# A two-layer graph kernel's head: row split ahead of the edge columns, first weights and packed rows loaded ahead, part of the edge table cleared on GpSimd

## The chip, the cores and the metric

The kernel runs on one core of one Trainium2 chip. A core has TensorE (PE in the profile, its weight loads PEld), VectorE (DVE), ScalarE (ACT), GpSimd (POOL), and SyncE (SP), which here issues DMAs. The metric is the device time of one execution in microseconds, lower is better. The kernel before took 1517.72 us, the median of three runs (1516.66 to 1518.28).

## The reference, cut to what matters

1250 nodes with 512 features pass through two layers. Each layer adds to `x` the sum of a graph branch (messages over 40,000 edges) and an attention branch, then a mixture-of-experts branch. What the change touches is the start of the first layer:

```
xn = layernorm(x)
neigh_mean = segment_sum(xn[src], dst) / max(deg, 1)
h = xn @ W_self.T + neigh_mean @ W_neigh.T + bias          # graph branch
a = layernorm(xn) * g1 + be1                               # attention branch
q = sigmoid(a @ Wq + bq); k = sigmoid(a @ Wk + bk); v = a @ Wv + bv
```

The second layer's graph branch uses the same edges with `edge_weight`. Edges come sorted by `dst`.

## The kernel before, in words

Nodes are handled in `T` = 10 tiles of `P` = 125 rows. The first stage makes five products for each tile: y (normalised x times the neighbour weights), z (times the self weights, plus a row vector), q, k and v (twice normalised x times their weights, plus row vectors). Each product is four matmuls of 128x512 in float32, which the trace shows as eight records.

In the same stage the edges become a dense table `at`, of 128 x 2 x 10 x 1258 float32: for each (source, target) pair the count of edges and the sum of weights. The 40,000 edges are 320 chunks of 125. For each chunk PE multiplies a one-hot matrix of sources (`hs`) with a matrix of targets (`hm`: one-hot, and one-hot times the weight in three bfloat16 parts), and DVE adds the result into 8 columns of `at` (L429). Chunks go in groups of eight: DVE makes `hs` (L387) and the one-hot of `hm` (L394), ACT scales a copy of it by the top part of the weight (L397), POOL by the two low parts (L400).

Before any chunk can start, DVE prepares the edges' columns (L326 to L359). Integer `dst` and `src` become float (`dst_f`, `src_f`); the least target of each chunk is taken (`base`); PE turns `src_f`, `dst_f` and the weights (`rest`) from rows of 500 into columns of 125 (L316), and DVE copies them out (`src_c`, `where`, `wt_e`, L317); ten compares give each edge's source tile (`tile_s`, L350 and L352), and from that come `lo_s`, `inside` and `col_w`. POOL splits the weights into bfloat16 parts (`w_low`, `w_top`, L345 to L349).

The biases and other row vectors come packed in a tensor of 16 rows, loaded three times into the partitions of `full` (L298). DVE splits them into three bfloat16 parts, `row_parts` (`split_rows`, L114 to L118: ten instructions). A row vector is added to a product by one more matmul, of `row_pick` with `row_parts` (L101). The first product that needs it is z of tile 0.

Each tile is normalised by DVE (`normal_rows`: statistics L246 and L247, an inverse root for which ACT takes the square root at L250, `xr` L267, a second root, `hr` L270), and turned on PE (`turn`, L132), from where ACT copies it to `xt` and, scaled, to `ht` (L278, L282). Tile 0 is done ahead of the edges' columns in the program; tile 1 when z of tile 0 begins; then one tile ahead. The statistics are taken for tiles 0, then 1 and 2, then 3 to 5, then 6 to 9 together.

`at` is cleared in 20 pieces of 128x1258, by ACT (L438): eight with `fill(8)` ahead of the loop, the rest four at a time.

PE's order in the product loop is the program's (a manual schedule). The order on the other engines, and on PE ahead of that loop, is made by a scheduler when the program is built, from dependences and its own estimates of time; so an instruction may stand somewhere else than the source suggests, and where an edit moves one, others move too. All loads of this stage are issued by SP, in order, with eight semaphores used in turn: a DMA waits until the one eight places ahead has landed. In the order before, these are x of tile 0 (two parts), `dst`, `src`, `rest`, `cols`, the neighbour weights, the self weights, then the three loads of the packed rows, x of tiles 1 and 2, and the weights of q, k and v.

Of the kernel before, what the change touches and what calls it, by code (L numbers as in the profile page):

```python
# [13 lines left out]
AF = mybir.ActivationFunctionType  # L14
# [21 lines left out]
NA = N + W  # L36
# [25 lines left out]
NROW = 16  # L62
# [8 lines left out]
def gps_two_layer_kernel(ctx: ExitStack, tc: tile.TileContext, x, src, dst, ew, rows, cols,  # L71
                         gw_self, gw_neigh, wq0, wk0, wv0, wo0, w1_0, w2_0, wg, we, be,
                         w_conv, w_lin, wq1, wk1, wv1, wo1, temp, w_r, w1_1, w2_1, b2_1, out):
    nc = tc.nc

    const = ctx.enter_context(tc.tile_pool(name="const", bufs=1))
    ident = const.tile([128, 128], F32, name="ident")
# [7 lines left out]
    row_parts = const.tile([96, D], BF16, name="row_parts")  # L85
    row_pick = const.tile([96, 32], BF16, name="row_pick")
    b2_parts = const.tile([96, D], BF16, name="b2_parts")
    cols_sb = const.tile([128, NCOL], F32, name="cols_sb")
# [5 lines left out]
    srcr = src.rearrange("(r e) -> r e", r=R)  # L94
    dstr = dst.rearrange("(r e) -> r e", r=R)
    ewr = ew.rearrange("(r e) -> r e", r=R)
# [12 lines left out]
    def split_rows(o, full, pool, **kw):  # L109

        piece = pool.tile([96, D], BF16, name="piece", **kw)
        back = pool.tile([96, D], F32, name="back", **kw)
        for i in range(3):
            nc.vector.tensor_copy(piece, full)  # L114
            nc.vector.tensor_copy(o[32 * i:32 * i + NROW, :], piece[32 * i:32 * i + NROW, :])
            if i < 2:
                nc.vector.tensor_copy(back, piece)
                nc.vector.tensor_tensor(full, full, back, ALU.subtract)  # L118
# [70 lines left out]
    at = adj.tile([128, 2, T, NA], F32, name="at")  # L189
# [3 lines left out]
    zero = l0.tile([128, 1], F32, name="zero")  # L193
# [16 lines left out]
    with ExitStack() as phase:  # L210
        gp = phase.enter_context(tc.tile_pool(name="gnn", bufs=1))
        ring = phase.enter_context(tc.tile_pool(name="ring", bufs=2))
# [16 lines left out]
        full = ring.tile([96, D], F32, name="full", tag="o", bufs=5)  # L229
# [43 lines left out]
        def turn(t):  # L273

            xr, hr = pairs[t]
            pt = transposed(ps, xr)
            xt = ring.tile([128, DC, P], F32, name="xt")
            nc.scalar.copy(xt, pt)  # L278
            pt = transposed(ps, hr)
            ht = ring.tile([128, DC, P], F32, name="ht")  # L280
            for c in range(DC):
                nc.scalar.activation(ht[:, c, :], pt[:, c, :], AF.Identity,  # L282
                                     bias=cols_sb[:, C_BE1 + c:C_BE1 + c + 1],
                                     scale=cols_sb[:, C_G1 + c:C_G1 + c + 1])
            turned[t] = xt, ht

        with tc.tile_pool(name="eprep", bufs=1) as ep, \
                tc.tile_pool(name="eps", bufs=2, space=PSUM) as eps:
            dst_i = ep.tile([R, RE], I32, name="dst_i")
            src_i = ep.tile([R, RE], I32, name="src_i")  # L290
            rest = ep.tile([R, RE], F32, name="rest")
            load_x(0)
            nc.sync.dma_start(dst_i, dstr)
            nc.sync.dma_start(src_i, srcr)
            nc.sync.dma_start(rest, ewr)
            nc.sync.dma_start(cols_sb, cols)
            for i in range(3):
                nc.sync.dma_start(full[32 * i:32 * i + NROW, :], rows[:NROW, :])  # L298
            wn_sb, ws_sb, wq_sb, wk_sb, wv_sb = (
                big[:, i * DC * D:(i + 1) * DC * D].rearrange("p (c f) -> p c f", c=DC)  # L300
                for i in range(5))
            for i, (o, w) in enumerate(((wn_sb, gw_neigh), (ws_sb, gw_self), (wq_sb, wq0),
                                        (wk_sb, wk0), (wv_sb, wv0))):
                nc.sync.dma_start(o, w.rearrange("(c p) f -> p c f", p=128))
                if i == 1:
                    load_x(1)
                    load_x(2)
            load_x(3)
            load_x(4)
            normal_rows(0)  # L310
            turn(0)

            def as_columns(o, f):
                pe = eps.tile([CH, NC // R, R], F32, name="pe")
                for j in range(NC // R):
                    nc.tensor.transpose(pe[:, j, :], f[:, j * CH:(j + 1) * CH], ident[:R, :R])  # L316
                nc.vector.tensor_copy(o.rearrange("p (r j) -> p r j", r=R), pe.rearrange("p j r -> p r j"))  # L317

            def chunks(ap):
                return ap.rearrange("r (j e) -> r j e", e=CH)  # L320

            def each_chunk(ap):
                return ap[:, :, None].to_broadcast([R, NC // R, CH])

            dst_f = ep.tile([R, RE], F32, name="dst_f")
            nc.vector.tensor_copy(dst_f, dst_i)  # L326
            src_f = ep.tile([R, RE], F32, name="src_f", tag="f", bufs=3)
            nc.vector.tensor_copy(src_f, src_i)
            src_c = ep.tile([CH, NC], F32, name="src_c")
            as_columns(src_c, src_f)  # L330
            base = ep.tile([R, NC // R], F32, name="base")
            nc.vector.tensor_reduce(base, chunks(dst_f), AX.X, ALU.min)

            nc.vector.tensor_scalar(base, base, 0.0, float(N - 1), op0=ALU.max, op1=ALU.min)
            nc.vector.tensor_copy(base_i, base)
            nc.vector.tensor_tensor(chunks(dst_f), chunks(dst_f), each_chunk(base), ALU.subtract)
            nc.vector.tensor_scalar(base, base, float(W), None, op0=ALU.add)
            out_f = ep.tile([R, RE], F32, name="out_f", tag="f", bufs=3)
            nc.vector.scalar_tensor_tensor(chunks(out_f), chunks(dst_f), float(W), each_chunk(base),
                                           op0=ALU.is_ge, op1=ALU.mult)  # L340
            nc.vector.tensor_add(dst_f, dst_f, out_f)
            as_columns(where, dst_f)
            as_columns(wt_e, rest)
            less = ep.tile([CH, NC], F32, name="less", tag="f", bufs=3)
            nc.gpsimd.tensor_copy(w_low[:, 0, :], wt_e)  # L345
            nc.gpsimd.tensor_copy(w_top, w_low[:, 0, :])
            nc.gpsimd.tensor_tensor(less, wt_e, w_top, ALU.subtract)
            nc.gpsimd.tensor_copy(w_low[:, 0, :], less)
            nc.gpsimd.tensor_tensor(w_low[:, 1, :], less, w_low[:, 0, :], ALU.subtract)  # L349
            nc.vector.tensor_scalar(tile_s, src_c, float(P), None, op0=ALU.is_ge)  # L350
            for t in range(2, T):
                nc.vector.scalar_tensor_tensor(tile_s, src_c, float(t * P), tile_s,  # L352
                                               op0=ALU.is_ge, op1=ALU.add)
            nc.vector.scalar_tensor_tensor(lo_s, tile_s, float(-P), src_c, op0=ALU.mult, op1=ALU.add)
            nc.vector.scalar_tensor_tensor(src_c, tile_s, float(W), where, op0=ALU.mult, op1=ALU.add)
            inside = ep.tile([CH, NC], F32, name="inside", tag="f", bufs=3)
            nc.vector.tensor_scalar(inside, where, float(W), None, op0=ALU.is_lt)
            nc.vector.scalar_tensor_tensor(src_c, src_c, 1.0, inside, op0=ALU.add, op1=ALU.mult)
            nc.vector.tensor_scalar(col_w, src_c, -1.0, None, op0=ALU.add)  # L359


            nc.vector.memset(row_parts, 0.0)
            split_rows(row_parts, full, ring, tag="o", bufs=5)
            for i in range(3):
                nc.vector.tensor_copy(row_pick[32 * i:32 * i + 32, :],
                                      ident[32 * i:32 * i + 32, 32 * i:32 * i + 32])


            worst = ep.tile([R, 1], F32, name="worst")
            nc.vector.tensor_reduce(worst, out_f, AX.X, ALU.max)  # L370
            pr = eps.tile([1, R], F32, name="pr", bufs=1)
            nc.tensor.transpose(pr, worst, ident[:R, :R])
            any_out = ep.tile([1, 1], F32, name="any_out")
            nc.vector.tensor_reduce(any_out, pr, AX.X, ALU.max)
            nc.vector.tensor_scalar(any_out, any_out, 0.0, float(NC), op0=ALU.is_gt, op1=ALU.mult)
            nc.vector.tensor_copy(trips, any_out)
# [54 lines left out]

        fills = [(m, t) for m in range(2) for t in range(T)]

        def fill(n):
            for _ in range(n):
                if fills:
                    m, t = fills.pop()
                    nc.scalar.activation(at[:, m, t, :], zero.to_broadcast([128, NA]), AF.Copy)  # L438

        kinds = ((y_d, 0, wn_sb, None, AF.Copy), (z_d, 0, ws_sb, R_GNN, AF.Copy),  # L440
                 (q_d, 1, wq_sb, R_BQ0, AF.Sigmoid), (k_d, 1, wk_sb, R_BK0, AF.Sigmoid),
                 (v_d, 1, wv_sb, R_BV0, AF.Copy))
        steps, step, chunk = T * len(kinds) * DC, 0, 0
        fill(8)
        with tc.manual_schedule(engines={mybir.EngineType.PE}):
            for t in range(T):
                for n, (d, which, w_sb, row, func) in enumerate(kinds):
# [39 lines left out]
        with tc.tile_pool(name="far", bufs=1) as fr, tc.tile_pool(name="fps", bufs=1, space=PSUM) as ps:  # L487
# [4 lines left out]
            with tc.For_i(0, n_far, 1) as i:  # L492
                i = nc.s_assert_within(i, 0, NC - 1)
# [942 lines left out]
```

## Time and profile before

| what | us |
|---|---|
| median of three runs | 1517.72 |
| the profiled execution | 1515.57 |
| its span, first to last instruction | 1513.9 |
| PE busy | 1389.8 (92%) |
| DVE busy | 586.5 (39%) |
| ACT busy | 404.4 (27%) |
| POOL busy | 199.1 (13%) |
| first edge product starts on PE | 41.86 |

The span is the time between the first and the last instruction in the profile; the execution's time has 1.67 us more around it. Busy shares are means over stages with different limits: in the first 40 us DVE is nearly always busy and PE is not, later it is the other way round. In the lines of the timeline the columns are start, duration, engine, source line, operation, what it writes and reads, and how often; in brackets stands the idle time ahead of it and what ended it. In the lines of waits: who waited, for whom, total us, how often, the longest. In the lines of windows: the stretch, its length, then for PE, PEld, DVE, ACT and POOL the busy us and the number of instructions, then PE's granted clock, the share of time that the DMA engines were busy, and GB/s.

### The profile page before, as it was taken

The numbers are of one execution on the slowest core, as the hardware profiler recorded it, in microseconds if no ns is written. First come the engines' busy times: TensorE is split into PE (matmuls) and PEld (weight loads), VectorE is DVE, ScalarE is ACT, GpSimd is POOL, SyncE is SP. The second block draws the span as 40 slices with busy tenths as digits, with TensorE's granted clock in tenths as the row PEclk, the third lists the DMA queues.
The fourth block names the chain that finished last, engine by engine and source line by source line (L and its number), as shares of the span: only waits on it lengthen the run. The fifth ranks groups of instructions, "written<-read, shape, count | busy, mean of one in ns | idle before, by whom it ended". The sixth has DMA issues, their size and how long they took to land. (4 is left out here: it accounts for less than half of the span.)

```text
span 1513.9 us, 18419 instructions
## 1 busy us (share of the span) xinstructions
PE 1389.8 (92%) x6082; PEld 870.1 (57%) x6082; DVE 586.5 (39%) x1425; ACT 404.4 (27%) x937; POOL 199.1 (13%) x176
## 2 busy tenths in 40 slices
PE   5999999999999699999965898898999999999997
PEld 2445445434544346554534696884767567975673
DVE  8887777689776583343575000000000000000000
ACT  8655455201224322112224111220212012120110
POOL 3345455300000000000005001000000000000000
PEclk9999999999999799999986999999999999999999
DMA  6311111623510130001149446601552106001011
GB/s 224 102 55 57 55 55 48 188 72 91 175 48 8 51 111 1 0 1 41 48 170 348 168 177 235 226 9 46 193 163 76 14 8 231 12 7 14 1 14 15
DMA packets 72716, 134.73 MB, mean 89 GB/s; under 512 B 8280, under 2 KB 9672, under 8 KB 72574
## 3 DMA queue, kind: packets, MB, share of 16 engines
q1 hardware_dynamic: 67646, 122.47, 23.9%
q0 software_dynamic: 4928, 10.43, 3.5%
q8 instruction: 81, 1.33, 0.4%
q14 instruction: 61, 0.50, 0.1%
HBM read 107.27 MB, written 26.38 MB: 88 GB/s over the span
## 5 line engine op out<-in xcount | busy, mean ns | idle before, releaser
L1323 PE MATMUL po<-w,big 128*128 128x512 f32 x576 | 250.1, 592 | 0.0
L1300 PE MATMUL pm<-hts,big 128*128 x960 | 184.7, 355 | 19.4 <-issue 17.0
L1312 DVE TENSOR_SCALAR o<-po,to_gate 128x512 f32<-128x512 f32 (+1 forms) x24 | 17.7, 749 | 453.8 <-PE po L1325 452.6
L1300 PEld LDWEIGHTS pm<-hts,big 128*128 128x128 f32 x960 | 167.0, 196 | 39.1 <-issue 23.8
L1323 PEld LDWEIGHTS po<-w,big 128*128 128x128 f32 x576 | 109.2, 190 | 132.0 <-issue 131.4
L1303 ACT ACTIVATE big<-pm,cols_sb 128x256 f32<-128x256 f32 (+2 forms) x224 | 96.1, 432 | 282.1 <-PE pm L1300 281.8
L1300 PE MATMUL pm<-hts,w 128*128 x832 | 144.7, 336 | 12.7 <-PEq L1383 5.8
L1300 PEld LDWEIGHTS pm<-hts,w 128*128 128x128 f32 x832 | 133.0, 197 | 23.9 <-issue 14.5
L455 PE MATMUL pm<-big,ht 128*125 128x512 f32 x240 | 130.5, 632 | 0.0
L1313 POOL DMA_INDIRECT out_dram<-o,row x24 | 36.9, 1539 | 650.5 <-DVE o L1312 285.2
L429 DVE TENSOR_TENSOR at<-at,pa 128x160 f32 x320 | 102.2, 319 | 41.3 <-PE pa L427 17.8
L400 POOL TENSOR_TENSOR hm<-hm,w_low 125x640 bf16<-125x640 bf16 x80 | 100.3, 1274 | 114.0 <-DVE hm L394 63.3
L123 PE MATMUL pm<-w,at 128*125 128x512 f32 x240 | 114.2, 598 | 0.0
L397 ACT ACTIVATE hm<-hm,w_top 125x80 bf16<-125x80 bf16 x320 | 86.4, 350 | 68.1 <-DVE hm L394 55.1
L633 PE MATMUL pn<-big,at 125*125 125x512 f32 x200 | 89.4, 604 | 3.0 <-DMA big<-q_d 3.0
L455 PE MATMUL pm<-big,xt 128*125 128x512 f32 x160 | 86.8, 633 | 1.2 <-ACT xt L278 1.2
L1303 ACT ACT_TABLE_LOAD x11 | 14.1, 1283 | 255.4 <-PE pm L1300 255.4
L427 PEld LDWEIGHTS <-hs 125*128 125x128 bf16 x640 | 50.8, 97 | 48.8 <-issue 44.0
L424 PE MATMUL pa<-hm,hs 125*128 125x160 bf16 x320 | 64.6, 233 | 12.9 <-DVE at L429 10.9
L424 PEld LDWEIGHTS <-hs 125*128 125x128 bf16 x320 | 31.1, 97 | 67.7 <-issue 38.4
L633 PEld LDWEIGHTS pn<-big,at 125*125 125x125 f32 x200 | 37.5, 191 | 52.5 <-issue 52.5
L427 PE MATMUL pa<-hm,hs 125*128 125x80 bf16 x640 | 64.4, 198 | 0.0
(391 smaller groups left out, 1616.1 us busy)
## 6 DMA issues: line engine op xcount, KB each, us to landing
w<-in_w_dram SPq DMA_DIRECT2D x52, 1024.0 KB
big<-in_w_dram SPq DMA_DIRECT2D x12, 1024.0 KB
x_t<-in_x_dram SPq DMA_DIRECT2D x10, 224.0 KB
xn_d<-xr SPq DMA_DIRECT2D x10, 224.0 KB
y_d<-o SPq DMA_DIRECT2D x10, 224.0 KB
z_d<-o SPq DMA_DIRECT2D x10, 224.0 KB
q_d<-o SPq DMA_DIRECT2D x10, 224.0 KB
k_d<-o SPq DMA_DIRECT2D x10, 224.0 KB
```

The source lines that it names most:

```text
L123: nc.tensor.matmul(ps, lhs[:, c, :], w[:, c, :], start=(c == 0), stop=(row is None and c == DC - 1))
L397: nc.scalar.activation(hm[:, j, 1, :], hm[:, j, 0, :], AF.Copy, scale=w_top[:, g * J + j:g * J + j + 1])
L400: nc.gpsimd.tensor_tensor(hm[:, :, 2 + i, :], hm[:, :, 0, :], w_low[:, i, c8, None].to_broadcast([CH, J, TW]), ALU.mult)
L424: nc.tensor.matmul(pa.rearrange("p k c -> p (k c)"), hs[:, j, :], hm[:, j, 0:2, :].rearrange("p k c -> p (k c)"), start=True, stop=False)
L427: nc.tensor.matmul(pa[:, 1, :], hs[:, j, :], hm[:, j, 2 + i, :], start=False, stop=(i == 1))
L429: add = nc.vector.tensor_tensor(to, to, pa.rearrange("p k (t w) -> p k t w", t=T), ALU.add)
L455: nc.tensor.matmul(pm, lhs[:, c, :], w_sb[:, c, :], start=(c == 0), stop=(row is None and c == DC - 1))
L633: nc.tensor.matmul(pn, at[:P, 0, s, t * P:(t + 1) * P], y[:, s, :], start=(s == 0), stop=(s == T - 1))
L1300: nc.tensor.matmul(pm[:, :width], w1s[e, f // DC][:, c, (f % DC) * 128:(f % DC + 1) * 128], hts[:, c, bass.ds(start, width)], start=(c == ...
L1303: nc.scalar.activation(hid[f][:, :width], pm[:, :width], AF.Gelu, bias=cols_sb[:, C_B11 + e * FC + f:C_B11 + e * FC + f + 1])
L1313: nc.gpsimd.indirect_dma_start(out, bass.IndirectOffsetOnAxis(ap=row[:n], axis=0), o[:n], None, bounds_check=N - 1, oob_is_err=False, comp ...
L1323: nc.tensor.matmul(pm, hid[f][:, s * 128:(s + 1) * 128], w2s[e, f // DC][:, f % DC, :], start=(f == 0), stop=False)
```

## The change

Three things are edited. The load of the neighbour weights is issued right behind x of tile 0, followed by `dst`, `src`, the three loads of the packed rows, the weights of the edges and the columns; before, the neighbour weights came behind all of these but the packed rows. The split of the packed rows, with its clear and the copies into `row_pick`, stands in the program ahead of the edges' columns and not behind them. The first eight of the 20 pieces of `at` are cleared by POOL and not by ACT.

The scheduler's order that follows from it, by the lists of both programs: SP issues the neighbour weights third, then `dst`, `src`, `rest`, `cols`, the self weights and the three packed-row loads, and what follows stays as it was. On DVE the conversions of `dst` and `src` stand behind `hr` of tile 0; the first piece of the split stands behind `worst` (L370), and the rest of the split alternates with `where`, `wt_e` and seven of the compares; the remaining compares, `lo_s`, `inside` and `col_w`, and `xr` of tile 1 come behind the last copy into `row_parts`; `xr` and `hr` of tile 3 come ahead of the first add into `at`. On PE `hr` of tile 0 is turned right behind `xr`, and all of product y of tile 0 stands between the turning of `src_f` and that of `dst_f`. On ACT the root for tiles 1 and 2 stands behind the copy of q of tile 0, with one more load of an activation table on each side, and the second root for them behind 14 scalings of `hm` and the copy of `xt` of tile 1. On POOL the eight clears stand between the clear of `full` and the casts of `w_low`.

```
             load_x(0)
-            nc.sync.dma_start(dst_i, dstr)
-            nc.sync.dma_start(src_i, srcr)
-            nc.sync.dma_start(rest, ewr)
-            nc.sync.dma_start(cols_sb, cols)
-            for i in range(3):
-                nc.sync.dma_start(full[32 * i:32 * i + NROW, :], rows[:NROW, :])
...
                 nc.sync.dma_start(o, w.rearrange("(c p) f -> p c f", p=128))
+                if i == 0:
+                    nc.sync.dma_start(dst_i, dstr)
+                    nc.sync.dma_start(src_i, srcr)
+                    for r in range(3):
+                        nc.sync.dma_start(full[32 * r:32 * r + NROW, :], rows[:NROW, :])
+                    nc.sync.dma_start(rest, ewr)
+                    nc.sync.dma_start(cols_sb, cols)
                 if i == 1:
                     load_x(1)
                     load_x(2)
             load_x(3)
             load_x(4)
             normal_rows(0)
             turn(0)
+
+            nc.vector.memset(row_parts, 0.0)
+            split_rows(row_parts, full, ring, tag="o", bufs=5)
+            for i in range(3):
+                nc.vector.tensor_copy(row_pick[32 * i:32 * i + 32, :],
+                                      ident[32 * i:32 * i + 32, 32 * i:32 * i + 32])
 
             def as_columns(o, f):
...
             nc.vector.tensor_scalar(col_w, src_c, -1.0, None, op0=ALU.add)
 
-            nc.vector.memset(row_parts, 0.0)
-            split_rows(row_parts, full, ring, tag="o", bufs=5)
-            for i in range(3):
-                nc.vector.tensor_copy(row_pick[32 * i:32 * i + 32, :],
-                                      ident[32 * i:32 * i + 32, 32 * i:32 * i + 32])
 
             worst = ep.tile([R, 1], F32, name="worst")
...
-        def fill(n):
+        def fill(n, early=False):
             for _ in range(n):
                 if fills:
                     m, t = fills.pop()
-                    nc.scalar.activation(at[:, m, t, :], zero.to_broadcast([128, NA]), AF.Copy)
+                    if early:
+                        nc.gpsimd.memset(at[:, m, t, :], 0.0)
+                    else:
+                        nc.scalar.activation(at[:, m, t, :], zero.to_broadcast([128, NA]), AF.Copy)
...
-        fill(8)
+        fill(8, early=True)
```

## The prediction

> **What bounds the kernel now.** I read the page first: TensorE (PE) is busy 92% of a span of 1513.9 us, so a change near the start can only move the time at which PE settles into its steady work. The change touches only the head: by the lists of instructions PE's order is the same from the self products on, and that of the other engines from some fifty instructions behind the first edge product. So I read who waited for whom up to 60 us, and the timeline of that stretch. Line numbers are those of the kernel before.
>
> ```profile
> PE pm L101 <- DVE row_parts L115: 6.9, 1, 6.9
> PE pt L132 <- DVE hr L270: 2.1, 1, 2.1
> ```
>
> Those are PE's two waits for VectorE (DVE). The timeline (start, duration, engine) shows what lies between them, and where the stage begins:
>
> ```profile
> 15.40 6.21 PE L455 MATMUL pm<-big,xt 128*125 128x512 f32 x14
> 28.16 0.28 DVE L115 COPY row_parts<-piece 16x512 bf16<-16x512 bf16 x1
> 28.50 0.58 PE L101 MATMUL pm<-row_parts,row_pick 96*125 96x512 bf16 x1 [6.89 <-DVE row_parts L115]
> 28.88 5.26 PE L455 MATMUL pm<-big,ht 128*125 128x512 f32 x8
> 31.62 1.55 DVE L267 TENSOR_SCALAR xr<-x_t,mv,r 125x512 f32<-125x512 f32 x1
> 36.86 0.65 PE L132 MATMUL pt<-ident,hr 125*128 125x125 f32 x4 [2.07 <-DVE hr L270]
> 37.34 3.60 PE L455 MATMUL pm<-big,ht 128*125 128x512 f32 x8
> 41.86 0.23 PE L424 MATMUL pa<-hm,hs 125*128 125x160 bf16 x1
> ```
>
> The reader is to see three things. PE stops at 21.61 and waits 6.9 us for the third copy into row_parts. The same eight records (four products) take 5.26 us after that stop and 3.60 us later: a PE that has stood still is slower at first, by 1.7 us. And DVE is late again right behind: the next turning needs xr and hr of tile 1. By windows of 10 us, 20 to 30 and 40 to 50:
>
> ```profile
> 20.00:30.00 10.00, 3.11 (x7) 1.39 (x6) 9.89 (x25) 7.99 (x10) 1.09 (x2) 0.77 0.73 248
> 40.00:50.00 10.00, 10.00 (x59) 5.11 (x58) 6.58 (x21) 4.94 (x14) 0.90 (x2) 1.00 0.50 143
> ```
>
> In the first DVE (third figure) is full and PE (first) is not; in the second PE is full. The head is DVE's, the stage behind it PE's. So the mark is the start of the first edge product, 41.86 us: what moves it moves the end one for one, since PE has no slack to absorb it.
>
> **The change part by part.** The lists of both kernels' instructions, engine by engine, show where the scheduler put things; I lay the changed lists out with the durations of the rows above and of their neighbours. DVE instructions that do not depend on each other start about 0.07 us before the one ahead ends (11.30 + 0.66, next at 11.88).
>
> *Loads.* The neighbour weights (1 MB) go ahead of dst, src, rest, cols. DMA waits show SP released by these weights at 9.72 and by the self weights at 13.20, so 1 MB takes 3.5 us. dst was there at 4.94; now at 8.4 or earlier, src, rest and cols each about 0.5 later. Their first users now start at 9.3 (dst), 10.5 (src), 12 (cols). Price 0; the cover is 0.9 us at dst. The packed rows are read by DVE at 15; a third load of them waits in SP for the neighbour weights (7 to 8 us), price 0. Everything behind them on SP (x tiles 1 and 2, the other weights) is used after 22.
>
> *DVE before the split.* The scheduler now puts dst_f, base and src_f (0.42 + 0.67 + 0.41) behind hr of tile 0. Before they filled DVE's wait for ScalarE's (ACT) square root at 7.15, which stays: three clears and two table loads stand ahead of it as before. ACT has one clear instead of two ahead of the second root, so hr ends at 9.4 (before 10.97). Then dst_f, three row_pick copies, base, src_f: 1.6, to 10.9 (before, src_f ended at 6.39). PE turns src (0.97), to 12.0. Thirteen more DVE instructions, the last the first piece of the split, lead to 15.4.
>
> *PE's list.* All four first products (8 records) now stand ahead of the turning of dst and rest; before, one did. 8 records are 3.5 at 0.43 each, from 12.0 (ACT's copy xt is there at 11.2), and one turning (0.4 until DVE may start on its four parts) follows. So DVE's copy "where", which was at 14.89, comes at 15.9; DVE waits 0.5 for it, with the split queued behind.
>
> *The split.* It is ten instructions; interleaved with columns the stretch from "where" to the third row_parts copy is 16 instructions, 6.1 us by their rows: 22.0 instead of 28.44. PE has ended the self products at 19.9. So the 6.9 us wait becomes 2.1.
>
> *What is late next.* The column work that was done before is now behind: from row_parts to the end of xr of tile 1 there are 22 instructions (three L352, inside, lo_s, two statistics, two hs at 1.2, two hm at 0.8 and small ones), 9.1 us: 31.1 instead of 33.17. Before it was 4.7. PE ends the q products at 26.2 and waits 5 us, where it waited 0.3. Of 6.4 us won, 2.1 are left. ACT's second root now stands behind 14 hm scalings and the copy of xt, and hr ends at 34.7, its turning at 34.8 (before 36.86): still 2.1. But PE has stood still for 5 us, so the k products take the slow 5.26 and not 3.60: 1.7 back. First edge product 42.2 against 41.86: **+0.4 us**, were no instruction stretched.
>
> *Stretched instructions.* In the trace before, DVE rows beside GpSimd (POOL) work are longer than their like:
>
> ```profile
> 18.00 1.04 DVE L352 SCALAR_TENSOR_TENSOR tile_s<-src_c,tile_s 125x320 f32<-125x320 f32 x1
> 19.95 0.87 DVE L115 COPY row_parts<-piece 16x512 bf16<-16x512 bf16 x1
> 30.48 1.21 DVE L253 TENSOR_TENSOR r<-mv,r 125x2 f32<-125x2 f32 x1
> 34.53 0.80 DVE L255 TENSOR_TENSOR r<-r,r 125x2 f32<-125x2 f32 x1
> ```
>
> Against 0.48, 0.28, 0.16, 0.16 elsewhere, with xr (1.55 against 0.54), piece (0.67 against 0.41) and two hr (1.41 against 1.0): 0.56 + 0.59 + 1.05 + 0.64 + 1.01 + 0.26 + 0.41 = 4.5 us. The 41.86 has these in it; my 42.2 does not. The POOL work that causes them (w_low at 16 to 21, hm from 29.6) is all still there, beside the split and the columns. **+4.5 us**; bounds 2 (it happens to meet fewer) and 6.
>
> *Eight clears on POOL.* POOL was idle 14.06 us ahead of its first cast, so its queue has room. One clear of 128x1258 by the row of another POOL clear (0.95 for 128x1024) is 1.17; eight, 9.4, from 2.1 to 11.5 or later, before wt_e. ACT loses 8 x 1.16, but ACT was waiting for DVE (2.01 us at 28.68): worth nothing there. The edge adds need all clears, long done. What the clears do to DVE is shown late in the trace:
>
> ```profile
> 783.19 0.17 DVE L1158 COPY count<-pcount 125x8 f32<-125x8 f32 x1
> 783.56 0.95 POOL L1144 MEMSET hts<- 128x1024 f32 x1
> 783.77 0.32 DVE L1166 TENSOR_TENSOR hotw<-hot,rank 125x160 f32<-125x160 f32 x1
> 784.01 0.53 DVE L1237 COPY planf<-base 125x8 f32<-125x8 f32 x1
> ```
>
> The copy ends with the clear (784.54 and 784.51). DVE has five copies or scalings that matter under the clears: xr, hr, dst_f, the first row_pick, src_f. Each is held for between 0 and 1.17, on average half: 5 x 0.58 = **+2.9 us** on DVE's chain. Bounds 0 and 5.9.
>
> The Trainium skill, SBUF — State Buffer, "Who interferes with whom", says that GpSimd and a DVE copy, cast or tensor_scalar in a two-port mode exclude each other for a whole instruction, while a clear, which reads nothing, does not hold a DVE operation with two inputs. The L1166 and L1237 rows agree. By that rule the five are held and nothing else: the same 2.9. The rule on the clock speaks against the change too: TensorE: Matmul & The Clock Gate, "What's actually happening", has PE at half rate after an idle window of some 3.4 us. By it, q (idle 2 to 4 us) might stay fast; by the 28.88 row, taken for k alone, 1.7. It makes no other term.
>
> Sum: 0.4 + 4.5 + 2.9 = **+7.8 us**. Profiled execution: 1515.57 (span 1513.9 and 1.67 around it) becomes 1523.4. The median of the runs, 1517.72, lies 2.15 above that execution; with the same shift it is **1525.5 us**, slower by 0.5%.
>
> **The rivals.** A measurement of this kernel tells about 0.2%, 3.0 us, from no change.
>
> *Faster.* The removed wait is won and nothing takes its place. Place: the end of xr of tile 1. If DVE got there as long after row_parts as before (4.7 us), the first edge product would be about 6 earlier: 1512. It decides when xr of tile 1 ends before 30. For it: the 6.9 us wait is real. Against: DVE is full from 10 to 34, the same instructions remain, and two idle stretches are added (before the first root, before "where"). Chance 0.07.
>
> *No change.* POOL meets only DVE operations it does not hold, or PE stays fast through the new stop: +0.4, or 42.2 + 2 to 4 less 1.7; 1518 to 1520. For it: the two-input columns ran beside the clear unhurt. Against: the 1.21 and 1.55 rows. Chance 0.10.
>
> *Much slower.* Upper bounds together with slow first products (8 records at up to 0.86, 3.4 more, with "where" and the split behind them): +0.4 + 4.5 + 5.9 + 1 or more, 1529.5 and above. For it: the first product record at 11.18 was slow, two records in 2.07. Against: the records at 15.40 were fast. Chance 0.08.
>
> **How the numbers follow.** The forecast (1521 to 1529) has 0.75. Slower is 0.75 + 0.08 = 0.83, same 0.10, faster 0.07. The range goes from 1518, which leaves out the faster case and half of the next, to 1529, which leaves out most of the last: under 0.2 in all.
>
> **What would show it.** In the profile of the changed kernel: the first row-vector product at 24 to 28 instead of 28.5; DVE waiting 0.5 to 3 us for PE at "where"; a PE wait of 4 us or more for xr of tile 1, a new one for its hr; xr and hr of tile 0 longer than 0.54; the k products near 5.2 us; the first edge product at 49 to 50. I am wrong if xr of tile 1 ends before 33 (then it is no slower), or if the gap between first edge product and end of the span, 1472 us now, shrinks.

## The result, and the profile after

The changed kernel took 1528.29 us, the median of six runs (1526.36 to 1531.22), against 1517.58 for six runs of the kernel before (1515.72 to 1520.27): a ratio of 1.0070, interval 1.0054 to 1.0087, slower by 0.7%. The profiled execution took 1531.22, the longest of the six; its span is 1529.5.

The timeline of PE answers to the lines shown of before (start, duration, engine, line, operation; in brackets the wait ahead of it). Line numbers are those of the changed kernel: L459 is the product line that was L455, L324 the turning of columns (L316), L425 the first edge product (L424).

```profile
11.16 1.07 PE L132 MATMUL pt<-ident,xr 125*128 125x125 f32 x4 [11.16 <-DVE r L254]
15.25 6.48 PE L459 MATMUL pm<-big,xt 128*125 128x512 f32 x8
21.57 0.56 PE L324 MATMUL pe<-ident,dst_f 80*125 80x80 f32 x4
30.45 0.38 PE L101 MATMUL pm<-row_parts,row_pick 96*125 96x512 bf16 x1 [4.30 <-DVE row_parts L115]
42.83 1.09 PE L132 MATMUL pt<-ident,xr 125*128 125x125 f32 x4 [6.65 <-DVE xr L267]
46.52 1.09 PE L132 MATMUL pt<-ident,hr 125*128 125x125 f32 x4 [2.60 <-DVE hr L270]
47.41 5.72 PE L459 MATMUL pm<-big,ht 128*125 128x512 f32 x8
54.06 0.23 PE L425 MATMUL pa<-hm,hs 125*128 125x160 bf16 x1
```

The first edge product starts at 54.06 instead of 41.86, 12.2 us later. The wait for `row_parts` has shrunk from 6.89 to 4.30, but it ends later than before (30.45 against 28.50), and a new wait of 6.65 for `xr` of tile 1 stands behind it. On POOL and DVE the timeline shows where the lateness begins:

```profile
1.98 8.76 POOL L440 MEMSET at<- 128x1258 f32 x8
7.46 3.55 DVE L267 TENSOR_SCALAR xr<-x_t,mv,r 125x512 f32<-125x512 f32 x1
11.93 0.55 DVE L270 TENSOR_SCALAR hr<-x_t,mv,r 125x512 f32<-125x512 f32 x1
22.17 0.49 DVE L325 COPY where<-pe 125x320 f32<-125x320 f32 x1 [3.25 <-PE pe L324]
30.11 0.28 DVE L115 COPY row_parts<-piece 16x512 bf16<-16x512 bf16 x1
41.22 1.55 DVE L267 TENSOR_SCALAR xr<-x_t,mv,r 125x512 f32<-125x512 f32 x1
```

`xr` of tile 0 takes 3.55 us instead of 0.54 and ends at 11.01, just behind the last clear (1.98 + 8.76 = 10.74). The copy `where` waits 3.25 us for PE, which is busy with the first product's eight records. Everything behind moves with it.

How far the lateness is carried shows in two answers on the line of the first edge products, of the kernel before and of this one (duration ns least, median, most; first and last start us):

```profile
L424 PE MATMUL pa<-hm,hs x320: 229/233/243, 41.9 to 290.1; 125*128 125x160 bf16 x160
```

```profile
L425 PE MATMUL pa<-hm,hs x320: 229/233/243, 54.1 to 302.0; 125*128 125x160 bf16 x160
```

From first to last it is 248.2 and 247.9: the edge stage passes the 12 us on whole. From the last of them to the end it is 1223.7 and 1227.5, so this execution lost 3.8 more there. Most of that belongs to the execution: second profiles of the two programs (below) have 1220.9 and 1223.5. Whether 2 or 3 us of it belong to the kernel these four profiles cannot say, as two of one kernel differ by that much.

### The profile page after: what moved, and what is told of

Same layout as the page of the kernel before. It is cut to its first block, busy times and chain, and to the rows that moved or that the text cites. A ratio compares the mean times of both kernels' runs of the same rounds, so it can differ in the third digit from the quotient of the medians.

```text
span 1529.5 us, 18424 instructions
## 1 busy us (share of the span) xinstructions
PE 1399.2 (91%) x6082; PEld 873.6 (57%) x6082; DVE 590.5 (39%) x1425; ACT 396.0 (26%) x929; POOL 209.8 (14%) x184
## 3 DMA queue, kind: packets, MB, share of 16 engines
q1 hardware_dynamic: 67646, 122.47, 23.7%
## 5 line engine op out<-in xcount | busy, mean ns | idle before, releaser
L459 PE MATMUL pm<-big,ht 128*125 128x512 f32 x240 | 132.7, 641 | 0.0
L459 PE MATMUL pm<-big,xt 128*125 128x512 f32 x160 | 88.8, 646 | 0.0
L425 PE MATMUL pa<-hm,hs 125*128 125x160 bf16 x320 | 64.6, 233 | 12.6 <-DVE at L430 10.5
L425 PEld LDWEIGHTS <-hs 125*128 125x128 bf16 x320 | 31.1, 97 | 67.4 <-issue 38.0
```

The source lines that it names most:

```text
L425: nc.tensor.matmul(pa.rearrange("p k c -> p (k c)"), hs[:, j, :], hm[:, j, 0:2, :].rearrange("p k c -> p (k c)"), start=True, stop=False)
L459: nc.tensor.matmul(pm, lhs[:, c, :], w_sb[:, c, :], start=(c == 0), stop=(row is None and c == DC - 1))
```

## The experiments

All kernels compute the whole reference. Each ratio is to runs of the kernel before on the same chip; chips differ (medians of the kernel before: 1512.96, 1517.93 and 1514.56 on the three used), so only ratios are compared across them. "Mark" is the start of the first edge product in the profile. Line numbers shift by a few from kernel to kernel. The theory was the prediction's: several delays on DVE's chain, each part of the change with its own. Rivals: one part makes the whole loss.

### One part at a time

The first run has the first hunk of the diff alone; the others are put together from the same hunks (loads, split, clears).

```
+                if i == 0:
+                    nc.sync.dma_start(dst_i, dstr)
...
+                    nc.sync.dma_start(cols_sb, cols)
```

> The kernel before with the move of the loads alone (neighbour weights first, then dst, src, packed rows, rest, cols). Three theories. Chain: the loss is a sum of delays on VectorE's chain, to which each of the three parts gives its own. Here nothing holds xr of tile 0, but dst_f, base and src_f stand behind hr and all four first products ahead of the turning of dst, as in the changed kernel. These products start 3.0 us earlier than in the changed kernel (xr not held), at 12.2, and take about 6.5, so the copy where comes at 19.1 against 14.89 before: first edge product near 46, about 1522 us (1520 to 1524). Clears alone: nothing, 1517 to 1519. Loads alone (the new order of the lists is the whole loss): first edge product near 54, 1526 to 1529.

Measured: mark 49.90, 1522.13 us, ratio 1.0059 (1.0044 to 1.0074).

> The kernel before with the move of the split alone. PE's list is that of before. Chain: the copy where stays near 15, the first row-vector product comes near 24, but xr of tile 1 now stands behind one more hs (1.2) and hm (0.8), so it ends near 35 instead of 33.2, PE has stood for some 6 us ahead of it and the k products take 5.3 instead of 3.6: 2.0 + 1.7 = 3.7 at most, about 1520.5 us (1518 to 1522). Clears alone or loads alone: 1517 to 1519. Split alone: 1526 to 1529.

Measured: mark 44.98, 1518.90 us, ratio 1.0037 (1.0024 to 1.0049).

> The kernel before with the eight clears on GpSimd alone. The list has six clears in a row and the last two between the casts of the edge weights. Chain: xr of tile 0 is held to the end of the sixth clear, 1.98 + 6 x 1.09 = 8.5, instead of ending at 8.0; the last two clears stretch VectorE's rows near 16 to 20 by up to 2: together 0.5 to 2.5, about 1519 us (1517.5 to 1520.5). Clears alone: 1526 to 1529. Loads alone or split alone: 1517 to 1519.

Measured: mark 45.01, 1520.98 us, ratio 1.0051 (1.0034 to 1.0067).

> The changed kernel with its clears back on ScalarE. Chain: xr of tile 0 takes 0.54 again, everything up to the copy where comes 3.0 earlier, and first edge product near 51 instead of 54: about 1525 us (1523 to 1527). Clears alone: 1517 to 1519. Loads alone or split alone: 1526 to 1529.

Measured: mark 49.53, 1522.75 us, ratio 1.0071 (1.0050 to 1.0092).

No rival holds: each part alone makes the kernel slower. The split is nearest to no change: its interval begins at 1.0024, and the kernel before gives 1.0015 against itself (below). By the mark the loads are the largest, +8.0 against +3.1 and +3.2, and beside them the split's place does nothing that shows (49.53 against 49.90). Each mark is that of one execution; where a program was profiled twice, the two differ by 0.2 (kernel before) and 2.25 (changed kernel). Two of the waits of the kernel with the loads alone (who, for whom, us in total, times, longest), up to 60 us:

```profile
DVE where L318 <- PE pe L317: 2.8, 1, 2.8
DVE bn L246 <- DMA x_t<-in_x_dram: 2.2, 1, 2.2
```

The second is the only wait for a DMA in that stretch, and it was 2.1 before: no engine waits for a transfer that was moved. But with `dst` and `src` behind the weights the scheduler puts `dst_f`, `base` and `src_f` behind `hr`, all of product y ahead of the turning of `dst_f`, and two `hs` and two `hm` ahead of `xr` of tile 1 (before, two `hs` and one `hm`). That its own estimate of landing times made it do so is inferred; the lists are what the runs show. PE's list in the head of this kernel is the changed kernel's. Its timeline:

```profile
12.06 5.71 PE L456 MATMUL pm<-big,xt 128*125 128x512 f32 x8
17.60 0.56 PE L317 MATMUL pe<-ident,dst_f 80*125 80x80 f32 x4
38.71 0.65 PE L132 MATMUL pt<-ident,xr 125*128 125x125 f32 x4 [3.39 <-DVE xr L267]
42.96 1.10 PE L132 MATMUL pt<-ident,hr 125*128 125x125 f32 x4 [3.60 <-DVE hr L270]
```

The eight records take 5.71, `dst_f` is turned 3.7 us later than before (13.88), and by `xr` of tile 1 the lateness has grown to 5.5 (37.10 against 31.62). `hr` of tile 1 is turned 6.1 later than before (42.96 against 36.86), and the k products behind it take 5.14 instead of 3.60.

The split alone shortens PE's wait for `row_parts` from 6.89 to 3.8, as the change says, but `xr` of tile 1 ends at 34.9 instead of 33.2: ahead of it DVE waits 1.59 for ACT's root, which now has the copy of q with its two table loads ahead of it.

```profile
28.43 1.28 ACT L463 ACT_TABLE_LOAD   x1
30.54 0.60 ACT L463 ACTIVATE o<-pm 125x512 f32<-125x512 f32 x1 [0.82 <-PE pm L101]
31.16 1.28 ACT L250 ACT_TABLE_LOAD   x1
32.45 0.20 ACT L250 ACTIVATE r<-r 125x2 f32<-125x2 f32 x1
```

The expected place was right, but to the extra `hs` and `hm` comes a wait for ACT. The other two combinations:

> The changed kernel without the move of the loads (split ahead, clears on GpSimd). The first four runs gave a first edge product at 49.90 for the loads alone, 44.98 for the split alone, 45.01 for the clears alone, 49.53 for loads and split, against 41.86 before and 54.06 in the changed kernel. Theory: the move of the loads makes the scheduler lay out other lists (first products ahead of the columns, more work ahead of xr of tile 1), and is the largest part. Then this kernel has 41.86 + 3.1 + 3.2 = 48.1, about 6 us of the loss less than the changed kernel, ratio to the kernel before 1.003 to 1.005. Rival: clears and split need no loads to do harm; first edge product 52 to 54, ratio 1.006 to 1.008.

Measured: mark 49.52, 1523.52 us, ratio 1.0046 (1.0030 to 1.0062). The size of the mark lies between the theory (48.1) and the rival (52 to 54); the ratio is inside the theory's.

> The changed kernel without the move of the split. The runs so far put the first edge product at 49.90 (loads alone) and 49.53 (loads and split): beside the moved loads the split's place does nothing. Theory: with the clears added, xr of tile 0 is held 3.0 again and all comes 3.0 to 4.5 later than with the loads alone: first edge product 53 to 54.5, ratio to the kernel before 1.006 to 1.008. Rival: the clears do their harm through the split (two casts more beside GpSimd); first edge product 50 to 51, ratio 1.004 to 1.005.

Measured: mark 50.97, 1525.63 us, ratio 1.0073 (1.0056 to 1.0090). The ratio is the theory's, the mark the rival's. The hold of 3.0 is there (`xr` of tile 0 takes 3.55), but the first products, which begin 3.0 later, then take 4.96 instead of 5.71, so `where` is 2.3 later and not 3.0 (20.46 against 18.20). By `xr` of tile 1 only 0.5 is left (37.63 against 37.10), as here the second `hm` (1.80 in the kernel with the loads alone) stands behind it and not ahead.

### The clears

With clears on POOL and no move of the loads, the first thing DVE has to do under them is the conversion of `dst`. In the kernels with the clears alone and with split and clears, six clears stand in a row:

```profile
1.98 6.58 POOL L439 MEMSET at<- 128x1258 f32 x6
5.17 3.66 DVE L326 CAST dst_f<-dst_i 80x500 f32<-80x500 int32 x1 [0.21 <-DMA dst_i<-in_dst_dram]
```

```profile
1.97 6.58 POOL L441 MEMSET at<- 128x1258 f32 x6
4.69 4.14 DVE L333 CAST dst_f<-dst_i 80x500 f32<-80x500 int32 x1 [0.24 <-DMA dst_i<-in_dst_dram]
```

The cast is there at 5.17 in one and at 4.69 in the other, and ends at 8.83 in both, 0.27 behind the last clear of the row (8.56 and 8.55). So it does not get in between two clears of 1.10; it waits for the row. The opposite edit keeps the row short:

```
-        fill(8, early=True)
+        fill(4, early=True)
+        fill(4)
```

> The changed kernel with four of the eight clears on GpSimd and four back on ScalarE; the lists of TensorE and VectorE are those of the changed kernel. Theory: a scaling of VectorE waits until the last of a row of clears ends, so with four (1.98 + 4 x 1.09 = 6.3) the scaling xr of tile 0, which is ready at 7.46, takes 0.54 instead of 3.55, and all that follows comes 3 earlier: copy where near 19, first edge product 50 to 51. Rival: the 3 us are absorbed further on by the waits for TensorE or ScalarE, or ScalarE's four more clears take their place: first edge product 53 to 54.

Measured: `xr` of tile 0 takes 0.54, the copy `where` comes at 18.68 and the mark at 50.33; 1524.17 us, ratio 1.0042 (1.0027 to 1.0057). The theory's numbers. Four clears, over at 6.38, hold nothing that DVE has ready.

### The order on PE

```
-            nc.tensor.transpose(pr, worst, ident[:R, :R])
+            turned_last = nc.tensor.transpose(pr, worst, ident[:R, :R])
...
+                        if step == 0:
+                            tc.add_manual_dep(mm.ins, turned_last.ins.name, NO_SYNC, reason="order")
```

> The changed kernel with one ordering added: the first product waits until the turnings of src, dst, rest and worst stand ahead of it on TensorE. Theory: the copy where waits 3.25 us for products that run slowly; without them it comes near 18.2 instead of 22.17, the third copy into row_parts 4 earlier, and the first edge product at 50 or, as ScalarE's list has the second root ahead of its table load too, earlier. Rival: from row_parts on it is the work ahead of xr and hr of tile 1 that counts and the products, now late, hold the first row vector: first edge product 53 to 54.

Measured: `where` at 18.84 instead of 22.17, the third copy into `row_parts` at 26.77 instead of 30.11, the mark at 49.48; 1525.21 us, ratio 1.0046 (1.0030 to 1.0063). The 3.3 us of `where` reach the mark (4.6 earlier; 2.3 against the 51.81 of the second profile below, where `where` came at 20.53), though by another way: the scheduler's lists behind `row_parts` changed too, PE waits 1.4 for `xr` of tile 1 and then 6.9 for `hr`, and the k products behind that stop take 6.21.

### Tile 1 ahead

```
             as_columns(wt_e, rest)
+            normal_rows(1)
...
-                    if n == 1 and t + 1 < T:
+                    if n == 1 and 0 < t and t + 1 < T:
                         normal_rows(t + 1)
```

Once in the kernel before with the split moved, once in the changed kernel.

> The kernel before with the split moved ahead (as in the change), and with the statistics, xr and hr of tile 1 written ahead of the columns' arithmetic instead of inside the loop; loads and clears as before. It is a try at a version that beats both. Theory: what sets the first edge product is when VectorE has made xr and hr of tile 1; they end near 29 and 32 here, TensorE has no stop over 3.4 us behind the row vector at 26 and the first edge product comes at 38 to 39, 3 to 4 us earlier than before, ratio 0.997 to 0.998. Rival: the targets hm, whose multiplications on ScalarE and GpSimd follow VectorE's, come too late instead: first edge product 41 to 43, ratio 0.999 to 1.001.

Measured: mark 35.27, earlier than either had it; 1517.26 us, ratio 0.9992 (0.9979 to 1.0005).

> The changed kernel, with the statistics, xr and hr of tile 1 written ahead of the columns' arithmetic; TensorE's list is that of the changed kernel. Theory: the mark is set by when VectorE has made xr and hr of tile 1, with TensorE slow behind its stop for them. xr and hr now end before the first row vector, which comes at 32 to 33 (30.45 and some 2 for the statistics ahead of it); q 5.3, turnings 1.1, k 3.6 and 1.6 more: first edge product 44 to 45.5 instead of 54.06, ratio to the kernel before 1.001 to 1.003. Rival: the targets hm, behind this work now, are late: first edge product 50 or later, ratio 1.004 to 1.007.

Measured: mark 40.18; 1521.22 us, ratio 1.0036 (1.0016 to 1.0055).

Both marks are earlier than the kernel before has it, and yet one kernel is no faster and the other is slower. The mark no longer says what the head costs. Edge products of the two (first and last start, as above):

```profile
L427 PE MATMUL pa<-hm,hs x320: 229/233/243, 35.3 to 286.2; 125*128 125x160 bf16 x160
```

```profile
L426 PE MATMUL pa<-hm,hs x320: 229/233/341, 40.2 to 294.5; 125*128 125x160 bf16 x160
```

The edge stage takes 250.9 and 254.3 instead of 248.2. In the second, PE starts the first chunk and then waits for the targets:

```profile
40.18 0.23 PE L426 MATMUL pa<-hm,hs 125*128 125x160 bf16 x1
41.17 0.20 PE L429 MATMUL pa<-hm,hs 125*128 125x80 bf16 x1 [0.76 <-POOL hm L402]
42.38 0.20 PE L429 MATMUL pa<-hm,hs 125*128 125x80 bf16 x1 [1.01 <-POOL hm L402]
```

The rival was right about it: POOL's multiplications of `hm` begin at 39.70 there. Ahead of them POOL's copy of `totals` takes 4.06 (0.61 in the kernel before): from 35.45 to 39.27 DVE makes two `hs` and two `hm`, and the copy ends at 39.73. In the first it is DVE's adds, for which PE waits 3.5 us between 36 and 70 (1.5 between 42 and 76 in the kernel before). By the last edge product the first is 3.9 ahead of the kernel before (286.2 against 290.1); of that about 1 is seen in the ratio. In its profile the gain is lost behind the edge stage: from there to the end it is 1229.9 against 1223.7, with a lower granted clock (0.77 against 0.89 from 285 to 300, 0.93 against 1.00 from 350 to 375, 0.91 against 1.00 from 460 to 480). Whether every execution loses it so isn't shown; the mean clock over the runs is 0.964 for both kernels. So this version matches the kernel before and, by their ratios, is 0.8 to 1.0% faster than the changed one; none of the kernels run is clearly faster than the kernel before.

### What repeats

> The changed kernel once more, to see what of its time repeats. Theory: the head is the same in every execution: first edge product 54.06 within 0.5; the gap from there to the end of the span, 1475.4 in the first profile, was longer than the 1472.0 of the kernel before by a stretch of slow clock near 478, which belongs to that execution: gap 1468 to 1476, ratio 1.006 to 1.008. Rival: the change itself lengthens the later stages: gap 1475 or more again.

Measured: 1527.49 us, ratio 1.0093 (1.0079 to 1.0108). Mark 51.81, not 54.06 within 0.5; gap 1471.5. The two profiles of the same program agree to 0.01 from `xr` of tile 0 to the first product, and part there:

```profile
15.25 4.84 PE L459 MATMUL pm<-big,xt 128*125 128x512 f32 x8
```

The same eight records take 4.84 here and 6.48 above. The kernel before does the same. In its first profile the 14 records from 15.40 on took 6.21, the row that the prediction read; in its second profile they are:

```profile
15.61 8.16 PE L455 MATMUL pm<-big,xt 128*125 128x512 f32 x14
```

There the wait for `row_parts` behind them takes up the difference, and the mark hardly moves (41.86 and 42.05). The clock record of these traces says when the records become fast. It has no entry for the first microseconds (the windows print 1.00 there); its first entry, of full clock, stands at 20.96 and 17.67 in the two profiles of the changed kernel and at 15.16 and 19.53 in those of the kernel before. Up to that time product records follow each other at 0.85 us or more, and right behind it, back to back, at 0.43; so it is in all 14 profiles. That the clock was at one half until then is inferred from the factor of two.

The stretch near 480 is the second difference; its windows (PE, PEld, DVE, ACT, POOL busy, granted clock, DMA share, GB/s) in the first profile and in this one:

```profile
480.00:490.00 10.00, 9.94 (x22) 4.63 (x23) 1.53 (x6) 3.48 (x6) 0.00 (x0) 0.74 0.00 0
```

```profile
480.00:490.00 10.00, 10.00 (x35) 5.09 (x34) 5.18 (x12) 4.47 (x10) 0.00 (x0) 1.00 0.01 2
```

A clock of 0.74 over 10 us is 5.2 us at half speed; with what lies before 480 the clock record of that trace has 6.8 us at one half there, which is 3.4 us lost, about what the gaps of the two profiles differ by (1475.4 and 1471.5). So the rival's 1475 did not come again. With gaps of 1472.0 and 1469.1 in the kernel before, a lengthening of 2 or 3 us is not ruled out.

> The kernel before against itself: ratio within 0.0015 of 1, first edge product 41.86 within 0.5, gap to the end of the span between 1467 and 1476. It shows what two equal kernels differ by.

Measured: ratio 1.0015 (1.0001 to 1.0029), mark 42.05, gap 1469.1. Two equal kernels can differ by 0.15%, 2.3 us. The table is to be read with that.

| kernel | mark | last edge product | ratio |
|---|---|---|---|
| before (again) | 41.86 (42.05) | 290.1 (290.3) | 1.0015 |
| split | 44.98 | 293.0 | 1.0037 |
| clears | 45.01 | 293.2 | 1.0051 |
| split, clears | 49.52 | 297.5 | 1.0046 |
| loads | 49.90 | 297.7 | 1.0059 |
| loads, split | 49.53 | 297.5 | 1.0071 |
| loads, clears | 50.97 | 298.4 | 1.0073 |
| changed kernel (again) | 54.06 (51.81) | 302.0 (299.8) | 1.0070 (1.0093) |

From first to last edge product it is 247.4 to 248.3 in every row. By the mark the parts do not add: 8.0 + 3.1 + 3.2 is 14.3, the whole is 10 to 12.2. The ratios follow the order of the marks roughly. For several kernels they are larger than the marks say, by 2.5 us for the split, 3.1 for loads and split and 4.6 for the clears. The granted clock goes with it: its mean over the runs on that chip is 0.967 for the kernel before and 0.965, 0.962 and 0.964 for these three, and 0.001 of clock over the span is 1.5 us of PE's time. PE's stops in the head take a part of that (by the clock records of the profiles 1.7 us more than in the kernel before ahead of the mark, 3.4 more, and none); why the rest is lost isn't shown.

## Why the prediction was right, and where its steps were not

The range, the sign and the chain were right. The time (1525.5; found 1528.29) was too low, and that it lies inside the range is partly luck: the upper end is 1529, and the ratio of the second series, 1.0093, would put it at 1531.7. The sum was too small, and the mark (49 to 50; found 54.06 and 51.81) shows by which terms. In the first profile 12.2 us divide as follows, against 0.4 + 4.5 + 2.9:

- **PE's list** is the term that was mis-sized most. It priced the eight records ahead of `dst_f` at 3.5, after the records at 15.40 of the trace before, so that "DVE waits 0.5". They took 6.48 (4.84 in the second profile, 4.8 to 6.0 in the experiments) and DVE waited 3.25: 3.0 us missing from the term of +0.4. The much slower rival had exactly this price, 3.4 with `where` and the split behind it. Its "Against", that the records at 15.40 were fast, was true of one execution: in the second profile of the same kernel, with PE at work since 8.15 as in the first, four of them take 0.85 to 0.93 each, and the fast ones begin at 19.75. So the row the price was taken from was a lucky one, and the record at 11.18 the nearer. With columns first the 3.3 us went away.
- **Eight clears** had the right size (3.0 against 2.9) for a wrong reason, which is luck. Not five operations were held for half a clear each, but one, `xr` of tile 0, for the rest of the row; the four others came when POOL was done. At the mark the hold is worth between 1.1 (loads, clears against loads) and 4.5 (changed kernel against loads, split), as the first products run faster or not and as the lists behind differ.
- **Stretched instructions** and what goes with them cost 5.4 instead of 4.5, inside the bounds. From `where` to the third copy it took 8.2 instead of 6.1 (L118 1.34, L114 1.01 beside `w_low`), and from there to the end of `xr` of tile 1 12.4 instead of 9.1 (`hm` 1.73, L253 1.21, `xr` 1.55 beside POOL's `hm`). Of the latter 0.56 is no stretching but a wait for ACT's root, which the sum did not have.
- **What is late next** was right in its place and its direction: a new wait for `xr` of tile 1 (6.65; worked out 5), one of 2.60 for its `hr` (2.07 before), k products slow at 5.72, and from `hr` to the mark 7.6 against 7.5 worked out.
- 0.4 + 3.0 (records) + 3.0 (clears) + 5.4 (stretched) is 11.8; 0.4 remains.
- **Loads** at "Price 0" was right for the transfers and misleading for the part: by the experiments this is the hunk whose lists cost the most, 8.0 us at the mark. The prediction had the lists' effect in its sum, but laid it to the order and not to the hunk that made it.
- **The first row-vector product** at 24 to 28 was wrong (30.45), by the 3.0 of the records, the 3.0 of the clears and 2.1 of stretching on top of the clean 22.0.
- **The mark moves the end one for one** holds roughly for losses (247.4 to 248.3 from first to last edge product, and the ratios above) and fails for gains: in the kernel with tile 1 ahead `xr` of tile 1 is done at 25.6, well before the 30 from which the faster rival decided, the mark came 6.6 earlier and the time stayed. That rival's 1512 was not to be had there.

The Trainium skill, SBUF — State Buffer, "Who interferes with whom", was the ground for half a clear each: whoever issues first has the shared ports for the whole instruction. The casts that end at 8.83 show more than one instruction's hold: behind the clear under way, two or three more passed ahead of a waiting DVE instruction. Here the measurement decides. TensorE: Matmul & The Clock Gate, "What's actually happening", says that the window in which PE's activity is judged runs freely, so that the moment of full speed falls differently in equal runs; 17.67 and 20.96 us in the two profiles of the changed kernel agree with it. The prediction used that page only for the stops and not for the start, where it spoke against the change.

## What to carry to other kernels

Where a scheduler orders the lists, an edit of one queue's order is an edit of all lists: build each part of a change alone and compare the lists before a price is put on it. Price the first matmuls of a kernel by the slow records unless several executions show them fast (here they became fast between 13.9 and 23.7 us, and at 15.16 and 19.53 in one program), and look at what is queued behind them. A mark that passes lateness on one for one need not pass earliness on; ask what the next engine has ready at the earlier time.

## What was not expected of the hardware

- A DVE cast or scaling waited out a whole row of GpSimd clears: from 4.69 and from 5.17 to the end of six clears at 8.56, from 7.46 to the end of eight at 10.74.
- A GpSimd copy waited out a row of DVE operations with two inputs: 4.06 us instead of 0.61, from 35.67 to 39.73, beside four of them from 35.45 to 39.27.
- Two executions of one program differ by 2.25 us at the first edge product (54.06 and 51.81), and it begins with 1.64 us in the first eight matmul records; a record goes from 0.85 to 0.43 at 20.96 in the one and at 17.67 in the other.
- The granted clock fell to one half for 6.8 us near 480 in one execution of the changed kernel and not in the other, at the cost of 3.4 us.
